# Weight loads as single steps, column means split up, block 1's norm and transposes closer together, and the exponential's table loaded ahead, in a fused graph-attention kernel

## The chip, the cores, the metric

One core of one Trainium2 chip. The metric is the device time of one launch in microseconds (us); smaller is better.

## The reference

128 graphs of 64 nodes with 768 features; two layers; the result is added to the input.

```python
h = relu(layernorm(x))
for l in range(2):
    m_left, m_right = h @ W_left[l].T, h @ W_right[l].T
    u_left, u_right = h @ m_left.T / sqrt(768), h @ m_right.T / sqrt(768)
    u = u_left * upper_triangle(adj) + u_right * lower_triangle(adj)
    e = exp(u) * adj
    attention = e / (sum(e, axis=2) + 1e-10)
    ctx = attention @ (h @ W_lin[l].T + b_lin[l])
    h = relu((ctx - mean) / (std + 1e-3) * ln_a[l] + ln_b[l])     # over features
out = x + h
```

## The kernel before

Each layer has two passes over 16 blocks of 512 tokens. Pass one multiplies by the left and the right weights and makes the scores; pass two multiplies by W_lin and forms the context. The products save matmuls by sums of blocks: fifteen products (ORDER) of sums of weight blocks and of token blocks (ts) into four PSUM tiles X, Y, Z, V, which ACT (ScalarE) or DVE (VectorE) read into m or hl. Pool (GpSimd) makes most of the sums. Nine raw 256 KB blocks make up a weight matrix; W_lin and the bias have their column mean taken off, so that the later norm needs no mean.

The order of the instructions is set by hand in slots, two to a group of eight matmuls. A slot runs what is planned for it, or else the next entry of a list for idle time:

```python
    def run(slot):
        if slot in plan:
            for f in plan.pop(slot):
                f()
        elif idle:
            f = idle.popleft()
            if f is not None:
                f()
```

The weights and the column means (t is the weight matrix in its nine blocks):

```python
        for s, (i, j) in RAW.items():
            nc.sync.dma_start(t[s], v[:, j * K2:(j + 1) * K2, i * D:(i + 1) * D])
        ...
            def means(blocks=blocks, m=m):
                for n, s in enumerate(blocks):
                    nc.vector.reduce_sum(m[:, n], t[s], axis=mybir.AxisListType.X)
                nc.vector.tensor_add(m[:, 0], m[:, 0], m[:, 1])
                nc.vector.tensor_add(m[:, 0], m[:, 0], m[:, 2])
                nc.vector.tensor_scalar_mul(m[:, 0], m[:, 0], 1.0 / H)
```

While block u is multiplied, block u+1 is prepared: statistics, norm, transposes into xb, a store of xb to memory (h) and a reload of it transposed (ht), then the row loads of block u+2 and an adjacency:

```python
            todo = transpose_rows(l, u, sp)          # statistics, norm, transposes, store
            todo.append(lambda: load_h(1, l, u))     # ht <- h
            if u + 1 < NB:
                todo.append(lambda: load_rows(l, u + 1, sp))
            todo.extend(softmax(u - 2) if u > 1 else [])
            todo.append(lambda: load_adj(u))
```

All these transfers go out from one queue (SP, SyncE) in program order. The slot at which one is written down sets its place in that queue, and no more: it goes out when the transfers before it have gone, the eighth before it has landed (the last row load for block 2 went out at 80.61, and the reload, eight places ahead, had landed at 80.59; of SP's 1238 transfers none went out before the eighth ahead of it had landed), and its own data are there (the reload went out at 73.44, and the store that it reads had landed at 73.29).

Of the kernel before, what the change touches and what calls it, by code (L numbers as in the profile page):

```python
# [17 lines left out]
def kernel(  # L18
# [27 lines left out]
    P = 128  # L46
# [69 lines left out]
    def load_w(l, kind):  # L116
        v = SRC[kind][l].rearrange("(c p) o -> p c o", p=P)
        t = W[l, kind] = [wpool.tile([P, K2, D], F32, name=f"w_{kind}_{s}") for s in range(len(ORDER))]
        for s, (i, j) in RAW.items():
            nc.sync.dma_start(t[s], v[:, j * K2:(j + 1) * K2, i * D:(i + 1) * D])  # L120

    def centre(l):

        t = W[l, "n"]
        for j in range(3):
            blocks = [s for s, (_, jj) in RAW.items() if jj == j]
            m = stat.tile([P, 3, K2], F32, name="wm", bufs=2)

            def means(blocks=blocks, m=m):
                for n, s in enumerate(blocks):  # L130
                    nc.vector.reduce_sum(m[:, n], t[s], axis=mybir.AxisListType.X)
                nc.vector.tensor_add(m[:, 0], m[:, 0], m[:, 1])
                nc.vector.tensor_add(m[:, 0], m[:, 0], m[:, 2])
                nc.vector.tensor_scalar_mul(m[:, 0], m[:, 0], 1.0 / H)

            idle.extend(none * (12 if j == 0 else 2))
            idle.append(means)
            for s in blocks:
                idle.extend(none * 3)
                idle.append(lambda s=s, m=m: nc.gpsimd.tensor_sub(  # L140
                    t[s], t[s], m[:, 0].unsqueeze(2).to_broadcast([P, K2, D])))

    def added(eng, o, sign, a, b):
        (eng.tensor_add if sign == "+" else eng.tensor_sub)(o, a, b)  # L144
# [114 lines left out]
    def transpose_rows(l, u, pool):  # L259

        key, xr, todo = (1, l, u), XR[l, u], []
        if l == 0:
            mv = stat.tile([P, Q, 2], F32, name="mv0", bufs=2)
            sd = stat.tile([P, Q], F32, name="sd0", bufs=2)
            rs = stat.tile([P, Q], F32, name="rs0", bufs=2)
            nb = stat.tile([P, Q], F32, name="nb0", bufs=2)

            def scale(q0, q1):
                nc.scalar.activation(sd[:, q0:q1], mv[:, q0:q1, 1], AF.Sqrt, bias=eps_in)
                nc.vector.reciprocal(rs[:, q0:q1], sd[:, q0:q1])  # L270
                nc.vector.scalar_tensor_tensor(nb[:, q0:q1], mv[:, q0:q1, 0], -1.0, rs[:, q0:q1],
                                               op0=ALU.mult, op1=ALU.mult)

            def norm(q):
                nc.scalar.activation(xr[q], xr[q], AF.Relu, bias=nb[:, q:q + 1], scale=rs[:, q:q + 1])

            stats = [lambda q=q: mean_var(mv[:, q, :], [xr[q][:, :HH], xr[q][:, HH:]]) for q in range(Q)]
            norms = [lambda q=q: norm(q) for q in range(Q)]
            if u:
                for f in stats + [lambda: scale(0, Q)] + norms:  # L280
                    todo.extend([f, None])
            else:
                scales = [lambda q=q: scale(q, q + 1) for q in range(Q)]
                todo.append(stats[0])
                for q in range(Q):
                    todo.extend(stats[q + 1:q + 2] + [scales[q], norms[q]])
        if (l, u) == (0, 0):
            ht = HT[key] = big.tile([P, C, T], F32, name="ht")

            def turn(c0):  # L290
                p = ps_aux.tile([P, 2, T], F32, name="aux")
                for c in range(2):
                    for q in range(Q):
                        nc.tensor.transpose(p[:, c, q * P:(q + 1) * P],
                                            xr[q][:, (c0 + c) * P:(c0 + c + 1) * P], ident)
                for c in range(2):
                    nc.scalar.copy(ht[:, c0 + c, :].rearrange("p (a g s) -> p g a s", a=4, g=2),
                                   p[:, c].rearrange("p (g a s) -> p g a s", a=4, g=2))

            for c in range(0, C, 2):  # L300
                todo.append(lambda c=c: turn(c))
            todo.append(lambda: nc.sync.dma_start(KEPT[l][u], ht))
            return todo

        xb = pool.tile([P, H // 32, Q, 32], F32, name="xb", bufs=1)

        def store():
            to = KEPT[l][u].rearrange("(b i) c t -> i c b t", b=4)
            for a in range(4):
                nc.sync.dma_start(to[:, :, :, a * P:(a + 1) * P],  # L310
                                  xb[a * 32:(a + 1) * 32].rearrange("i (c b) q j -> i c b (q j)", b=4))

        for q in range(Q):
            todo.append(lambda q=q: nc.vector.transpose(
                xb[:, :, q, :], xr[q].rearrange("p (b j) -> p b j", j=32)))
            todo.append(None)
        todo.append(store)
        return todo

# [6 lines left out]
    def pass_one(l, aside):  # L326
        with tc.tile_pool(name=f"one{l}", bufs=2, reuse_waits="tile") as sp:
# [106 lines left out]
            if l == 0:  # L434
                load_rows(0, 0, sp, (nc.sync, nc.scalar))
                warm = stat.tile([P, 1], F32, name="warm", bufs=1)
                nc.scalar.activation(warm, eps_in, AF.Sqrt)
                load_w(0, "l")
                load_w(0, "r")
                for f in transpose_rows(0, 0, sp):  # L440
                    if f:
                        f()

                t, w = deque(sums_t((1, 0, 0), nc.vector)), deque(sums_w(0, "l", nc.vector))
                needs = ("twww", "t", "wt", "ttwww", "wwww", "w", "tw", "t", "ww", "ww", "", "t", "t", "t", "t")
                for i, what in enumerate(needs):
                    for f in [(t if c == "t" else w).popleft() for c in what]:
                        if i < 3:
                            f()
                        else:  # L450
                            just.setdefault(i - 3, []).append(f)
                assert not t and not w
            load_adj(0)
            load_rows(l, 1, sp)
            if l == 0:
                cols.extend([column("a_col", ln_a[0]), column("b_col", ln_b[0])])
            for u in range(NB):
                slot = 0
                if u == 0:
                    if l == 0:  # L460
                        rs = sums_w(0, "r", nc.gpsimd)

                        def hold():

                            t = stat.tile([P, 1], F32, name="hold", bufs=1)
                            nc.gpsimd.tensor_copy(t, M[0][:, 0, 4, 0, :1])

                        put(16, hold)
                        for n in range(0, len(rs), 3):
                            put(17 + n // 3, *rs[n:n + 3])  # L470
                    slot = 14
                if u + 1 < NB:
                    slot = put_all(slot, prepare(u + 1))
                    nxt = (1, l, u + 1)
                else:
                    put(8, lambda: load_h(2, l, 0))
                    slot = put_all(9, softmax(u - 1) + none * 4 + affine(2, l, 0))
                    nxt = (2, l, 0)
                assert slot <= 47
                put_sums_t(nxt, max(slot, 40), 2 if slot <= 40 else 1, 30)  # L480
                if u in aside:
                    aside[u]()
                for k in range(2):
                    project(u, k, just if k == 0 and u == 0 else {})
                assert not plan
# [15 lines left out]
    def bias(l):  # L501
# [4 lines left out]
            row(f"b{i}", b_lin[l], i * D, (i + 1) * D, t[:, to])  # L506
        bm = stat.tile([P, 3], F32, name="bm", bufs=1)

        def centred():
            nc.vector.reduce_sum(bm, t[:, :3], axis=mybir.AxisListType.X)  # L510
            nc.vector.tensor_add(bm[:, 0:1], bm[:, 0:1], bm[:, 1:2])
            nc.vector.tensor_add(bm[:, 0:1], bm[:, 0:1], bm[:, 2:3])
            nc.vector.tensor_scalar_mul(bm[:, 0:1], bm[:, 0:1], -1.0 / H)
            nc.vector.tensor_scalar_add(t[:, :3], t[:, :3], bm[:, 0:1])

        def combined():
            nc.vector.tensor_add(t[:, 1], t[:, 1], t[:, 0])
            nc.vector.tensor_add(t[:, 3], t[:, 1], t[:, 2])
            for n in (0, 2):
                nc.vector.tensor_scalar_mul(t[:, n], t[:, n], -1.0)  # L520

        later([centred, combined], 6)
        return t

    AHEAD = []
# [158 lines left out]

    def one_aside(l):
        def begin():
            load_w(l, "n")
            centre(l)
            later(sums_w(l, "n", nc.gpsimd), 3)
            rows["bias", l] = bias(l)  # L690
# [1 line left out]

    def two_aside(kind):
        def begin():
            load_w(1, kind)
            later(sums_w(1, kind, nc.gpsimd), 4)
        return begin

    pass_one(0, {1: one_aside(0)})
# [32 lines left out]
```

## Time and profile before

| | before |
|---|---|
| time, median of the first 3 runs | 2802.0 us (2799.4 to 2802.6) |
| PE busy, of a profiled span of 2803.0 us | 2755.9 us |
| a block of pass one without a hole | 56.1 us |
| a slot | 0.86 us |

PE (TensorE) is busy nearly throughout, so what counts is where it stands still. A way of reading: block u's score matmuls come in one burst (tile aux) at the head of block u+1's work, so the distance from one burst to the next is the time of one block, and whatever is above 56.1 us is a hole. A burst is 192 matmuls with 192 weight loads, 384 instructions in 4.2 us. PE's program is fetched while it runs: the instruction queue (q8 of the page) moved 149 packets of 16.4 KB, and the trace holds 38111 instructions of PE, its sequencer's included. That makes blocks of some 256 instructions, an estimate that takes all of q8 for PE's; by it a burst uses up more than one of them. An "issue" wait is one for which the profile shows no semaphore.

### The profile page before, as it was taken

How to read it: one execution, taken by the hardware profiler on the slowest of the kernel's cores; microseconds unless marked ns; L12 is line 12 of the kernel's file. 1: busy time of each engine (PE TensorE's matmuls, PEld its weight loads, DVE VectorE, ACT ScalarE, POOL GpSimd, SP SyncE). 2: the span in 40 equal slices, each digit the busy share in tenths (PEclk: the TensorE clock that was granted, in tenths of full speed). 3: DMA queues.
4: the chain of work that ended last, by engine and by line, in shares of the span. 5: the costliest groups of instructions: out<-in, count | busy, mean ns of one | idle time of the engine just before them, and what ended most of it. 6: DMA issues, size and time to landing. Idle time of an engine off the chain costs nothing.

```text
span 2803.0 us, 46102 instructions
## 1 busy us (share of the span) xinstructions
PE 2755.9 (98%) x18712; PEld 2342.4 (84%) x18712; DVE 1340.9 (48%) x2223; ACT 838.7 (30%) x1452; POOL 1190.1 (42%) x935
## 2 busy tenths in 40 slices
PE   7999999999999999999999999999999999999997
PEld 6788888888888888888788888888888888888885
DVE  6454554454544332232345434443444335666666
ACT  2123222322131244444522221212122214545443
POOL 3343333222322556555333353223222335887875
PEclk9999999999999999999999999999999999999999
DMA  5633343234322243343563432343234204555654
GB/s 155 164 78 74 94 115 87 74 88 119 88 74 76 98 141 117 106 130 106 149 160 97 120 79 74 91 119 85 74 85 118 69 25 145 162 169 158 184 162 125
DMA packets 234068, 310.80 MB, mean 111 GB/s; under 512 B 54144, under 2 KB 184448, under 8 KB 225664
## 3 DMA queue, kind: packets, MB, share of 16 engines
q1 hardware_dynamic: 233568, 307.06, 40.0%
q8 instruction: 149, 2.44, 0.4%
q10 hardware_dynamic: 288, 0.79, 0.1%
q14 instruction: 63, 0.52, 0.1%
HBM read 202.91 MB, written 104.86 MB: 110 GB/s over the span
## 4 chain that ended last, share of the span: by engine, by line
PE 94%; DVE 2%; DMA 1%; ACT 1%; issue 1%; SPq 0%; POOL 0%; DVEq 0%; ACTq 0%; POOLq 0%
PE X L366 23%; PE V L366 15%; PE X L637 12%; PE Y L366 11%; PE Z L366 8%; PE V L637 8%; PE Y L637 6%; PE aux L392 5%; PE Z L637 4%; PE aux L564 3%; DVE m L144 1%; DMA ht<-h 0%; DMA h<-xb 0%; ACT ht L255 0%; DVE w_l L144 0%
## 5 line engine op out<-in xcount | busy, mean ns | idle before, releaser
L144 POOL TENSOR_TENSOR ts<-ht 128x512 f32<-128x512 f32 x441 | 585.7, 1340 | 1242.1 <-DMA ht<-h 555.7
L189 ACT ACTIVATE m<-X 128x512 f32<-128x512 f32 x256 | 152.7, 596 | 1117.1 <-PE X L366 589.5
L144 POOL TENSOR_TENSOR ts<-ht,ts 128x512 f32<-128x512 f32 x189 | 248.9, 1325 | 152.8 <-PE X L637 75.9
L144 DVE TENSOR_TENSOR m<-m,V 128x512 f32<-128x512 f32 x256 | 174.4, 681 | 271.9 <-PE V L366 271.9
L144 DVE TENSOR_TENSOR m<-m,X 128x512 f32<-128x512 f32 x256 | 163.8, 682 | 250.2 <-PE X L366 249.5
L366 PE MATMUL X<-ts,w_l 128*128 128x256 f32 x1024 | 246.6, 384 | 6.0 <-DVE w_l L144 2.1
L637 PE MATMUL X<-w_n,ts 128*128 128x256 f32 x1024 | 244.2, 380 | 0.9 <-ACT hl L189 0.6
L366 PE MATMUL X<-ts,w_r 128*128 128x256 f32 x1024 | 242.1, 379 | 0.2 <-ACT m L189 0.2
L144 DVE TENSOR_TENSOR m<-m,Z 128x512 f32<-128x512 f32 x128 | 88.0, 688 | 318.3 <-ACT m L189 257.3
L366 PEld LDWEIGHTS X<-ts,w_l 128*128 128x128 f32 x1024 | 194.2, 192 | 38.5 <-DVE m L144 4.6
L637 PEld LDWEIGHTS X<-w_n,ts 128*128 128x128 f32 x1024 | 191.6, 190 | 32.2 <-DVE hl L144 2.3
L366 PEld LDWEIGHTS X<-ts,w_r 128*128 128x128 f32 x1024 | 192.2, 190 | 29.6 <-ACT m L189 0.6
L255 ACT ACTIVATE ht<-ht,b_col,a_col 128x512 f32<-128x512 f32 x192 | 144.1, 808 | 142.9 <-DMA ht<-h 142.9
L637 PE MATMUL Y<-w_n,ts 128*128 128x256 f32 x768 | 182.4, 379 | 0.0
L366 PE MATMUL Y<-ts,w_l 128*128 128x256 f32 x768 | 181.8, 380 | 0.0
L366 PE MATMUL Y<-ts,w_r 128*128 128x256 f32 x768 | 181.4, 379 | 0.0
L189 ACT ACTIVATE hl<-X 128x512 f32<-128x512 f32 (+1 forms) x136 | 77.9, 573 | 329.4 <-PE X L637 320.0
L366 PEld LDWEIGHTS Y<-ts,w_l 128*128 128x128 f32 x768 | 146.4, 191 | 20.0
L637 PEld LDWEIGHTS Y<-w_n,ts 128*128 128x128 f32 x768 | 145.9, 190 | 19.8
L366 PEld LDWEIGHTS Y<-ts,w_r 128*128 128x128 f32 x768 | 145.9, 190 | 19.8
L603 POOL TENSOR_TENSOR z<-z,b 128x768 f32<-128x768 f32 x64 | 115.4, 1816 | 94.9 <-DVE z L600 94.9
L144 DVE TENSOR_TENSOR hl<-hl,X 128x512 f32<-128x512 f32 (+1 forms) x136 | 83.1, 653 | 147.2 <-PE X L637 139.8
(106 smaller groups left out, 4684.8 us busy)
## 6 DMA issues: line engine op xcount, KB each, us to landing
ht<-h SPq DMA_DIRECT2D x63, 1536.0 KB, 7.2
h<-xb SPq DMA_DIRECT2D x124, 384.0 KB, 6.8
z<-z SPq DMA_DIRECT2D x128, 192.0 KB, 2.9
x<-z SPq DMA_DIRECT2D x128, 192.0 KB, 8.4
xr<-in_x_dram SPq DMA_DIRECT2D x128, 192.0 KB, 3.7
out_dram<-xr SPq DMA_DIRECT2D x128, 192.0 KB, 2.6
x<-in_x_dram SPq DMA_DIRECT2D x120, 192.0 KB, 8.4
adj<-in_adj_dram SPq DMA_DIRECT2D x64, 128.0 KB, 2.8
```

Of the source, the lines that this page charges most:

```text
L144: (eng.tensor_add if sign == "+" else eng.tensor_sub)(o, a, b)
L189: nc.scalar.activation(to(o), p, AF.Copy, scale=1.0 if sign == "+" else -1.0)
L255: nc.scalar.activation(ht, ht, AF.Relu, bias=cols[1][:, c:c + 1], scale=cols[0][:, c:c + 1])
L366: nc.tensor.matmul(p[:, g], w[ORDER[i][0]][:, c, g * P:(g + 1) * P], b()[t][:, c, :], start=(new and g == c == 0), stop=(c == K2 - 1), ski ...
L392: nc.tensor.matmul(p[h * S + e:h * S + e + 32, q, e:e + 96], ht[:, c, b * S + e:b * S + e + 32], mb[:, e:e + 96], start=(c == 0), stop=(c ...
L564: nc.tensor.matmul(cx[k][i, m, :HH], at[j, q, :], hl[j, q, m * HH:(m + 1) * HH], start=True, stop=True)
L603: nc.gpsimd.tensor_add(zs[k], zs[k], rows["b"])
L637: nc.tensor.matmul(p[:, n], b[t][:, c, r * P:(r + 1) * P], w[s][:, c, :], start=(i in FIRST and i not in PRELOAD and n == c == 0), stop=(c ...
```

## The change

Its intent: to take four kinds of clump out of the schedule. Weight loads go one by one into idle slots instead of nine in a row; the three reductions of a column mean and the bias's steps get a slot each; block 1, which is prepared in a hurry, loses the empty slots between its norms and its transposes; the exponential's table in layer 1 is loaded by a dummy activation ahead of its first use.

```diff
     def load_w(l, kind):
-        for s, (i, j) in RAW.items():
-            nc.sync.dma_start(t[s], v[...])
+        return [lambda s=s, i=i, j=j: nc.sync.dma_start(t[s], v[...]) for s, (i, j) in RAW.items()]
...
-            idle.extend(none * (12 if j == 0 else 2))
-            idle.append(means)
+            def mean_of(m=m, mean=mean):
+                nc.vector.reduce_sum(mean, m.rearrange("p n c -> p c n"), axis=mybir.AxisListType.X)
+                nc.vector.tensor_scalar_mul(mean, mean, 1.0 / H)
+            idle.extend(none * (6 if j == 0 else 2))
+            for n, s in enumerate(blocks):
+                idle.append(lambda ...: nc.vector.reduce_sum(m[:, n], t[s], axis=mybir.AxisListType.X))
+            idle.append(mean_of)
...
-                for f in stats + [lambda: scale(0, Q)] + norms:
+                for f in stats + [lambda: scale(0, Q)]:
                     todo.extend([f, None])
+                for f in norms:
+                    todo.extend([f] + none * (u > 1))
...                                                  # after each transpose
-            todo.append(None)
+            todo.extend(none * ((l, u) != (0, 1)))
...                                                  # pass one, layer 1
+                warm = stat.tile([P, 1], F32, name="warm", bufs=1)
+                put(8, lambda: nc.scalar.activation(warm, eps_in, AF.Exp))
...                                                  # bias
-        later([centred, combined], 6)
+        later([mean, centred, combined, lambda: negated(0), lambda: negated(2)], 3)
...                                                  # pass one, then pass two
-            load_w(l, "n")
+            later(load_w(l, "n"), 1)
...
-            load_w(1, kind)
-            later(sums_w(1, kind, nc.gpsimd), 4)
+            later(load_w(1, kind), 1)
+            later(sums_w(1, kind, nc.gpsimd), 3)
```

(Not shown: in `bias`, two additions of single columns become one small reduction, and the two negations become functions of their own.)

More of the change, by code (lines that the diff above doesn't have):

```diff
@@ L118, in load_w @@
         t = W[l, kind] = [wpool.tile([P, K2, D], F32, name=f"w_{kind}_{s}") for s in range(len(ORDER))]
-        for s, (i, j) in RAW.items():
-            nc.sync.dma_start(t[s], v[:, j * K2:(j + 1) * K2, i * D:(i + 1) * D])
+        return [lambda s=s, i=i, j=j: nc.sync.dma_start(t[s], v[:, j * K2:(j + 1) * K2, i * D:(i + 1) * D])
+                for s, (i, j) in RAW.items()]
     def centre(l):
@@ L127, in centre @@
             m = stat.tile([P, 3, K2], F32, name="wm", bufs=2)
-            def means(blocks=blocks, m=m):
-                for n, s in enumerate(blocks):
-                    nc.vector.reduce_sum(m[:, n], t[s], axis=mybir.AxisListType.X)
-                nc.vector.tensor_add(m[:, 0], m[:, 0], m[:, 1])
-                nc.vector.tensor_add(m[:, 0], m[:, 0], m[:, 2])
-                nc.vector.tensor_scalar_mul(m[:, 0], m[:, 0], 1.0 / H)
-            idle.extend(none * (12 if j == 0 else 2))
-            idle.append(means)
+            mean = stat.tile([P, K2], F32, name="wmm", bufs=2)
+            def mean_of(m=m, mean=mean):
[3 more added lines that the diff above has]
+            for n, s in enumerate(blocks):
+                idle.append(lambda n=n, s=s, m=m: nc.vector.reduce_sum(m[:, n], t[s], axis=mybir.AxisListType.X))
+            idle.append(mean_of)
             for s in blocks:
                 idle.extend(none * 3)
-                idle.append(lambda s=s, m=m: nc.gpsimd.tensor_sub(
-                    t[s], t[s], m[:, 0].unsqueeze(2).to_broadcast([P, K2, D])))
+                idle.append(lambda s=s, mean=mean: nc.gpsimd.tensor_sub(
+                    t[s], t[s], mean.unsqueeze(2).to_broadcast([P, K2, D])))
     def added(eng, o, sign, a, b):
@@ L437, in pass_one @@
                 nc.scalar.activation(warm, eps_in, AF.Sqrt)
-                load_w(0, "l")
-                load_w(0, "r")
+                for f in load_w(0, "l") + load_w(0, "r"):
+                    f()
                 for f in transpose_rows(0, 0, sp):
@@ L456, in pass_one @@
                 cols.extend([column("a_col", ln_a[0]), column("b_col", ln_b[0])])
+            else:
+                warm = stat.tile([P, 1], F32, name="warm", bufs=1)
+                put(8, lambda: nc.scalar.activation(warm, eps_in, AF.Exp))
             for u in range(NB):
@@ L507, in bias, with mean @@
         bm = stat.tile([P, 3], F32, name="bm", bufs=1)
+        bs = stat.tile([P, 1], F32, name="bs", bufs=1)
+        def mean():
+            nc.vector.reduce_sum(bm, t[:, :3], axis=mybir.AxisListType.X)
+            nc.vector.reduce_sum(bs, bm, axis=mybir.AxisListType.X)
         def centred():
-            nc.vector.reduce_sum(bm, t[:, :3], axis=mybir.AxisListType.X)
-            nc.vector.tensor_add(bm[:, 0:1], bm[:, 0:1], bm[:, 1:2])
-            nc.vector.tensor_add(bm[:, 0:1], bm[:, 0:1], bm[:, 2:3])
-            nc.vector.tensor_scalar_mul(bm[:, 0:1], bm[:, 0:1], -1.0 / H)
-            nc.vector.tensor_scalar_add(t[:, :3], t[:, :3], bm[:, 0:1])
+            nc.vector.tensor_scalar_mul(bs, bs, -1.0 / H)
+            nc.vector.tensor_scalar_add(t[:, :3], t[:, :3], bs)
         def combined():
@@ L518, in combined, with negated @@
             nc.vector.tensor_add(t[:, 3], t[:, 1], t[:, 2])
-            for n in (0, 2):
-                nc.vector.tensor_scalar_mul(t[:, n], t[:, n], -1.0)
-        later([centred, combined], 6)
+        def negated(n):
+            nc.vector.tensor_scalar_mul(t[:, n], t[:, n], -1.0)
+        later([mean, centred, combined, lambda: negated(0), lambda: negated(2)], 3)
         return t
```

## The prediction

> **What bounds the kernel now.** I read the page first: which engine is full, and what the chain that ended last is made of.
>
> ```profile
> PE 2755.9 (98%) x18712; PEld 2342.4 (84%) x18712; DVE 1340.9 (48%) x2223; ACT 838.7 (30%) x1452; POOL 1190.1 (42%) x935
> ...
> PE 94%; DVE 2%; DMA 1%; ACT 1%; issue 1%; SPq 0%; POOL 0%; DVEq 0%; ACTq 0%; POOLq 0%
> ```
>
> TensorE is busy for 98% of the span and makes 94% of the chain. No part of the change touches a matmul: the built programs have the same PE instructions in the same order. So only holes in PE can be won, and 2803.0 - 2755.9 = 47 us is all the idle time there is. The view of waits for PE says whose they are (total, times, longest):
>
> ```profile
> PE aux L294 <- ACT x L275: 12.1, 4, 8.7
> PE V L366 <- DVE m L144: 3.9, 3, 1.5
> PE Z L366 <- issue: 3.1, 1, 3.1
> ...
> PE X L366 <- POOL ts L144: 2.1, 1, 2.1
> ...
> PE X L366 <- DVE m L144: 1.2, 1, 1.2
> ```
>
> The largest is the start, which the change leaves alone. The others are single events. To find them I took the chain in order of time and measured from one burst of score matmuls (aux) to the next, one burst per block of pass one:
>
> ```profile
> 83.97 4.10 PE aux L392 x192
> ...
> 146.18 4.10 PE aux L392 x192
> ...
> 203.58 4.10 PE aux L392 x192
> ...
> 259.68 3.60 PE aux L392 x168
> ```
>
> A good block takes 259.68 - 203.58 = 56.1 us. The distance from block 1's burst to block 2's is 62.2 (6.1 too long), the next 57.4 (1.3 too long). By the same view the one from 372.30 to 430.19 is 57.9 (1.8), in layer 1 those from 1464.47 to 1522.41 (1.8) and from 1747.79 to 1805.01 (1.1). Pass two repeats every 29.2 us almost without a hole. Four lines show what is inside: the timelines of PE, DVE and ACT and the stretch from 91 to 98 us (PE, PEld, DVE, ACT, POOL busy; clock; DMA share; GB/s).
>
> ```profile
> 92.44 1.65 PE L366 MATMUL Z<-ts,w_l 128*128 128x256 f32 x3 [3.10 <-issue]
> ```
> ```profile
> 91.00:98.00 7.00, 5.56 (x13) 4.48 (x14) 2.92 (x7) 1.06 (x2) 4.80 (x5) 0.51 0.70 241
> ```
> ```profile
> 194.37 1.19 DVE L133 TENSOR_TENSOR wm<-wm 128x2 f32<-128x2 f32 x1
> ```
> ```profile
> 1481.89 1.28 ACT L412 ACT_TABLE_LOAD   x1
> ```
>
> In block 1 PE stands 3.1 us with no semaphore to blame, after five of eight matmuls, and then runs at half clock. In the second a tiny addition for the column means takes 1.19 us on DVE, in front of PSUM reads. In the third the exponential's table is loaded in the middle of a block.
>
> [...] queue 8 moved 2.44 MB in 149 packets, 16.4 KB each. [...] a 2.1 us hole at 81.97 left the clock at 1.00. [...] the load took 1.28 us here, and exp began 0.02 us after it[...].
>
> **The change part by part.**
>
> *Norm and transposes of block 1 closer.* Four empty slots go among the norms and four among the transposes (a slot is 0.86 us, half a group of 1.73 us). The norms ran back to back anyway (ACT, 49.65 to 53.44), held by late statistics. The last transpose ended at 62.56; DVE is free from 52.5 on, needs 4 x 0.97 us and lets one PSUM read in, so it can end near 57.4, 5.15 us earlier. Behind it stands a chain of transfers: the store issued at 62.58 landed at 73.29, the reload of ht issued at 73.44 landed at 80.59, Pool's first sum began at 80.66, and PE waited 2.11 us for it, to 81.97. Five us of lead remove this wait and the restart: **2.35 us** (X can begin at 79.87 and the burst at 81.6 instead of 83.97).
>
> *Weight loads one by one.* Read packet by packet, the fetch for the PE block that block 1's burst uses up started at 89.99 and took 1.02 us; PE went on 1.43 us later. In four blocks without DMA load that fetch starts 1.1 to 1.7 us after the burst begins; here it would have been about 85.3. It was 4.7 us late: it stood behind transfers issued before it (the weight load issued at 83.35 landed at 89.75, the next at 90.53). The 3.1 us, and 14 matmuls at 0.427 instead of 0.216 us after it (3.0 us), make block 1's 6.1.
> The name of this part promises more than the program does. SP issues when its own queue lets it: nothing ties a load to the slot. In the built program the three bias rows and six of the nine loads still stand directly behind block 1's adjacency and go out at once; only three fall behind block 2's. So I work it out: all of SP's stream moves 5.15 us forward, PE's burst 2.35. The fetch is asked for near 82.95. The last adjacency lands at 89.34 - 5.15 = 84.2, the bias rows add 3 x 0.35, two weight loads 2 x 0.66: the fetch starts near 86.3, ends 87.3, PE goes on near 88.7, and needs it at 89.34 - 2.35 = 87.0. A wait of 1.7 us is left[...]. Worth (3.1 - 1.7) + 3.0 = **4.4 us**. In pass two and layer 1 the loads cost no PE time before (no hole beside them), so nothing there.
>
> *Column means in single steps.* Per third of the matrix three reductions (0.6 us each) stay, two tiny additions and a scaling become one reduction and a scaling: 6 DVE instructions fewer, in all 8 of 2223 with the bias. What counts is the clump: from 191.61 to 195.76 DVE did 4.15 us without reading PSUM, and V waited 0.93 us at 196.41. Split: **1.2** of that block's 1.3 us. The bias (0.94 + 3 x 0.16 + 0.62, five instructions in one slot at 393.31) stood between transposes and cost V 1.43 us at 400.6. Split and one block later, two additions (0.85 us) still stand before a transpose; counting DVE's work from 391.84 on gives V's read ending at 399.6 against 399.17 wanted: 0.45 left, **1.3 us** of 1.8. In layer 1 the bias additions (1755.39 to 1756.68) delayed a store and reload of ht; they move to late slots: **0.9** of 1.1.
>
> *Exponential's table ahead.* The load delayed exp, the product with exp waited 2.5 us on DVE, a PSUM read stood behind it, and X waited 1.2 us at 1485.89. Early in layer 1's block 0 ACT is idle 2.85 us between reads and hides 1.28: **1.5** of 1.8.
>
> Sum: 2.35 + 4.4 + 1.2 + 1.3 + 0.9 + 1.5 = 11.65 us; I take 0.5 off for new small holes. 2802.0 - 11.2 = **2791 us**, 0.4% less.
>
> **Rivals.** *The fetch still waits long.* Six loads and three bias rows still go out with the burst. If the fetch is again over 4 us late, 3.1 us and the half clock stay: 2795. If, on the contrary, the lead takes it past the backlog, there is no wait: 2789. For the first speaks that DMA is full throughout (share 1.08 from 80 to 90); for the second that bias rows are smaller.
> *The single steps fill slots that are already full.* Three reductions now stand at slots 1, 3 and 5 of block 2 beside the statistics: between the reads of Z and Y DVE then has 0.69 + 2 x 0.6 + 2 x 1.1 = 4.1 us of work where two groups give 3.46. That makes a read 1.2 us late, but that PSUM bank is next written four groups on. If I misjudge such clumps in three or four blocks: 2794 to 2796.
> *Loads that come later make a consumer wait in order.* The last three loads stand behind block 2's adjacency, near 135; DVE reduces them near 144 after block 2's burst at 139. They should be there by 139. They can also delay block 2's fetch, about 1 us with 1.3 to spare. If a reduction waits, DVE stands and PE with it: 2 to 4 us back.
>
> **Range and chances.** All removable holes together are about 14 us (2788), and with none of the fetch's gain and two misjudged clumps it is 2797. Runs of the kernel before spread over 3.1 us. So 2786 to 2797. Two per cent are 56 us, more than all of PE's idle time, so faster by 2% can't come from this: 1%. Slower by 2% would need a transfer or an order gone badly wrong: 0.5%.
>
> **What would show it.** Right: no PE wait for Pool's ts near 80; the burst of block 1 near 81.6; the "issue" wait of Z at 1 to 2 us and clock 1.00 after it; distances between bursts near 57.8, 56.2, and for the three others 56.1 to 56.6; no table load beside exp in layer 1. Wrong: half clock again near 90; ht landing later than 76; a new wait of PE for DVE's m in block 2 or 3; DVE waiting for a weight load; more than 50 us of PE idle.

## The result

The changed kernel took 2792.4 us (median of 4 runs, 2790.6 to 2793.3) against 2801.0 (4 runs) of the kernel before, and 2791.3 (5 runs) against 2801.7 (9 runs) when it was run again. The ratios are 0.9968 (95% interval 0.9951 to 0.9986) and 0.9961 (0.9947 to 0.9974). A ratio is the mean time of one kernel's fast runs over that of the other's of the same rounds, so not quite the ratio of the medians quoted.

The page of the changed kernel, busy times and chain:

```profile
PE 2751.3 (99%) x18712; PEld 2340.8 (84%) x18712; DVE 1340.8 (48%) x2215; ACT 837.8 (30%) x1453; POOL 1191.5 (43%) x935
...
PE 95%; issue 1%; DVE 1%; POOL 1%; DMA 1%; ACT 1%; SPq 0%; DVEq 0%; ACTq 0%; POOLq 0%
```

The work is the same; the span is 11.4 us shorter than that of the first trace of before. Its view of waits for PE (us in total, times, longest):

```profile
PE aux L297 <- ACT x L276: 12.3, 4, 8.9
...
PE Z L369 <- issue: 1.5, 1, 1.5
PE V L369 <- DVE m L145: 1.5, 1, 1.5
...
PE X L369 <- POOL ts L145: 1.1, 1, 1.1
```

Of three waits of V for DVE one is left, in block 0, which the change does not touch. X's wait for DVE's m in layer 1 is gone. The wait for Pool is 1.1 us, not gone. The issue wait has halved. The chain of the changed kernel in order of time, its first bursts:

```profile
83.17 4.10 PE aux L395 x192
...
141.07 4.10 PE aux L395 x192
...
197.16 4.10 PE aux L395 x192
...
253.26 3.60 PE aux L395 x168
```

141.07 - 83.17 = 57.9 us instead of 62.2, and 56.1 instead of 57.4 for the next. PE's timeline after the burst, and the stretch from 91 to 98 us:

```profile
90.08 0.92 PE L369 MATMUL Z<-ts,w_l 128*128 128x256 f32 x3 [1.54 <-issue]
```
```profile
91.00:98.00 7.00, 7.00 (x34) 6.15 (x34) 3.82 (x11) 3.28 (x6) 4.04 (x5) 1.00 0.04 13
```

The clock stays at 1.00, and DMA is quiet (share 0.04) where it was at 0.70. Which part of the change did that? SP's timeline around the burst shows the order in which the transfers went out (start, us of the whole row):

```profile
68.02 0.35 SPq L249 DMA_DIRECT2D ht<-h  x1
68.46 11.65 SPq L244 DMA_DIRECT2D x<-in_x_dram  x8
80.50 1.31 SPq L341 DMA_DIRECT2D adj<-in_adj_dram  x2
81.86 1.55 SPq L506 DMA_DIRECT2D bias<-in_b_lin_dram  x3
83.46 3.16 SPq L119 DMA_DIRECT2D w_n<-in_w_lin_dram  x6
```

Six of nine weight loads still go out in one run of 3.2 us, beside the burst (83.17 to 87.27): "one by one in free slots" holds in the program's text, not in time.

### The profile page after: what moved, and what is told of

Same layout as the page of the kernel before. It is cut to its first block, busy times and chain, and to the rows that moved or that the text cites. A ratio compares the mean times of both kernels' runs of the same rounds, so it can differ in the third digit from the quotient of the medians.

```text
span 2791.6 us, 46094 instructions
## 1 busy us (share of the span) xinstructions
PE 2751.3 (99%) x18712; PEld 2340.8 (84%) x18712; DVE 1340.8 (48%) x2215; ACT 837.8 (30%) x1453; POOL 1191.5 (43%) x935
## 4 chain that ended last, share of the span: by engine, by line
PE 95%; issue 1%; DVE 1%; POOL 1%; DMA 1%; ACT 1%; SPq 0%; DVEq 0%; ACTq 0%; POOLq 0%
PE X L369 23%; PE V L369 15%; PE X L648 12%; PE Y L369 12%; PE Z L369 8%; PE V L648 8%; PE Y L648 6%; PE aux L395 5%; PE Z L648 4%; PE aux L575 3%; POOL w_r L145 1%; DVE wm L409 0%; DMA x<-in_x_dram 0%; DMA w_r<-in_w_right_dram 0%; DMA w_l<-in_w_left_dram 0%
## 5 line engine op out<-in xcount | busy, mean ns | idle before, releaser
L145 POOL TENSOR_TENSOR ts<-ht,ts 128x512 f32<-128x512 f32 x189 | 249.3, 1327 | 154.7 <-PE X L648 76.9
```

The costliest lines, as they stand in the source:

```text
L145: (eng.tensor_add if sign == "+" else eng.tensor_sub)(o, a, b)
```

## The experiments

Eleven runs. First the four parts each alone on the kernel before, then both kernels again, then one part left out and mends. The table puts their traces side by side: the wait of PE for Pool ahead of block 1's burst, the issue wait after it, and the time from burst to burst (start to start; blocks are counted by the burst that opens the stretch; "L1" is layer 1). Two rows are read packet by packet from the traces: how long after the burst's start the instruction fetch that it needs begins, and how long block 1's reload of ht takes from issue to landing. Two runs, late_loads and late2_gap2, stand in the text only.

| us | before | before again | close | loads | steps | table | after | after again | at once | gap | late2 |
|---|---|---|---|---|---|---|---|---|---|---|---|
| wait for Pool | 2.1 | 1.8 | 0 | 1.6 | 1.5 | 1.5 | 1.1 | 0 | 0.9 | 0 | 0 |
| issue wait | 3.1 | 2.6 | 1.4 | 2.2 | 2.6 | 2.4 | 1.5 | 0.5 | 1.2 | 1.2 | 0 |
| fetch begins after | 6.1 | 5.8 | 4.5 | 5.2 | 5.6 | 5.6 | 4.6 | 3.6 | 3.1 | 4.1 | 2.1 |
| reload of ht takes | 7.2 | 6.8 | 7.9 | 6.8 | 6.9 | 6.7 | 11.8 | 10.1 | 11.6 | 7.0 | 9.0 |
| 1 to 2 | 62.2 | 59.0 | 57.7 | 58.6 | 59.0 | 58.7 | 57.9 | 56.9 | 57.6 | 57.6 | 56.1 |
| 2 to 3 | 57.4 | 57.6 | 57.5 | 56.1 | 56.5 | 57.3 | 56.1 | 56.1 | 56.1 | 56.1 | 56.1 |
| 6 to 8 | 114.0 | 114.2 | 114.4 | 113.1 | 112.4 | 114.4 | 113.2 | 113.3 | 113.1 | 113.2 | 113.0 |
| L1, 1 to 2 | 57.9 | 57.9 | 58.1 | 57.9 | 57.7 | 56.6 | 56.3 | 56.6 | 56.3 | 56.3 | 56.3 |
| L1, 6 to 8 | 113.7 | 114.0 | 113.4 | 112.6 | 112.6 | 112.9 | 112.9 | 112.9 | 113.1 | 112.6 | 112.6 |
| median time | 2801 | 2801 | 2797.2 | 2795.8 | 2798.1 | 2799.5 | 2792.4 | 2791.3 | 2793.0 | 2792.4 | 2789.7 |

Single traces carry chance: small issue waits of 0.2 to 0.7 us inside other bursts come and go, so a difference under 0.5 us in one cell says nothing.

### Only the closer norm and transposes

```diff
 # on the kernel before
-                for f in stats + [lambda: scale(0, Q)] + norms:
+                for f in stats + [lambda: scale(0, Q)]:
                     todo.extend([f, None])
+                for f in norms:
+                    todo.extend([f] + none * (u > 1))
...
-            todo.append(None)
+            todo.extend(none * ((l, u) != (0, 1)))
```

> Only the closer norm and transposes of block 1, on the kernel before; all nine weight loads and the bias rows still go out at once behind block 1's adjacency. My theory: the instruction fetch that PE needs after block 1's score burst waits behind the transfers issued before the burst began, so what helps it is how far the transfers' stream moves ahead of PE, not how many loads follow. Then this part alone brings most of block 1's 5.1 us: burst at 83 instead of 84, fetch starting near 87.7, the issue wait 1 to 2 us instead of 3.1, no half clock, and 4.5 to 5.5 us off the span (2795.5 to 2796.5). Rival (the change's own intent): nine loads in a row hold the fetch up; then the wait stays at 3 us or grows to over 4, because the burst comes earlier than before, half clock stays, and only 0 to 1 us is won. The holes near 196, 400, 1486 and 1784 stay in both.

Measured: 2797.2 us, ratio 0.9985 (0.9971 to 0.9999), some 4 us, a little under the 4.5 to 5.5 that I had expected. From its waits for PE:

```profile
PE Z L368 <- issue: 1.4, 1, 1.4
...
PE X L368 <- DVE m L144: 1.2, 1, 1.2
```

There is no wait for Pool any more, and with all nine weight loads and the bias still sent at once the issue wait is 1.4 us, as in the full change. The rival (more loads, longer wait) is out. What followed the burst in the queue made no wait of 3 us here; how far the queue had got by then is what this run changed.

### Only the weight loads as single steps

```diff
 # on the kernel before
-            load_w(l, "n")
+            later(load_w(l, "n"), 1)
...
-            idle.extend(none * (12 if j == 0 else 2))
+            idle.extend(none * (6 if j == 0 else 2))
...
-            load_w(1, kind)
-            later(sums_w(1, kind, nc.gpsimd), 4)
+            later(load_w(1, kind), 1)
+            later(sums_w(1, kind, nc.gpsimd), 3)
```

> Only the weight loads as single steps (with the shorter pause ahead of the column means), on the kernel before. My theory: the bias rows and six loads still go out at once beside the burst at 84, and the fetch stands behind what was issued before it; the wait stays 2.5 to 3.1 us with half clock after it, and the kernel gains 0 to 0.7 us. Rival (intent): three loads fewer beside the burst and small bias rows first let the fetch through: wait under 1.5 us, no half clock, 4 us or more off the span.

Measured: 2795.8 us, ratio 0.9983 (0.9970 to 0.9995). Of the fetch, the wait is nearer my theory than the rival, but outside the range of either: 2.2 us where I had written 2.5 to 3.1 and the rival had under 1.5; and the half clock that I had expected did not come. And the kernel gained near 5 us where I had written 0 to 0.7, for a reason that I had not thought of: loads in the idle list push everything behind them to other slots. The column means of the three thirds are still three clumps, but they stand elsewhere: they begin at 141, 180 and 210 us instead of 116, 156 and 192. Two lines of the second one in DVE's timeline:

```profile
180.13 1.86 DVE L131 TENSOR_REDUCE wm<-w_n 128x2 f32<-128x512 f32 x3
...
182.09 0.16 DVE L133 TENSOR_TENSOR wm<-wm 128x2 f32<-128x2 f32 x1
```

Its second tiny addition takes 0.16 us; in the clump that made the hole of the kernel before (at 192) it took 1.19. None of the three makes PE wait for DVE now, and the hole from burst 2 to 3 is gone (56.1), without any splitting. The bias's clump has moved too: 6 to 8 loses 1 us, L1 6 to 8 loses 1.1 us. So most of the time credited to "loads" is won by moving DVE's work. (The edit also shortens two pauses in the list; the run cannot tell their share of the shift from that of the loads' entries.)

### Only the column means and the bias in single steps

```diff
 # on the kernel before: the changed kernel's centre() and bias(), with the pause of 12 kept
-            idle.append(means)
+            for n, s in enumerate(blocks):
+                idle.append(lambda ...: nc.vector.reduce_sum(m[:, n], t[s], axis=mybir.AxisListType.X))
+            idle.append(mean_of)
...
-        later([centred, combined], 6)
+        later([mean, centred, combined, lambda: negated(0), lambda: negated(2)], 3)
```

> Only the column means and the bias in single steps, on the kernel before. My theory: block 1 stays as it was (wait 2.1 for Pool, 3.1 issue, half clock); the DVE holes near 196 (0.9 us) and 400 (1.4 us) and the late reload near 1780 in layer 1 go: distances between bursts of 57.4, 57.9 and 57.2 fall to 56.1 to 56.7, together 2.5 to 3.3 us off the span. Rival: PE's reads only wait elsewhere, as DVE does nearly the same work: under 1 us.

Measured: 2798.1 us, ratio 0.9986 (0.9974 to 0.9999), about 3 to 4 us. Block 1 stays (issue wait 2.6), the three stretches fall to 56.5, 112.4 and 112.6. Its waits of V for DVE:

```profile
PE V L367 <- DVE m L145: 1.7, 2, 1.5
```

The two that are left are block 0's 1.5 us and a new one of 0.2 us near 168, where a reduction now stands. For the holes this is as expected, and the rival (they only move) holds for 0.2 us; the half clock that I had expected in block 1 did not come.

### Only the table ahead

```diff
 # on the kernel before, pass one, layer 1
+            else:
+                warm = stat.tile([P, 1], F32, name="warm", bufs=1)
+                put(8, lambda: nc.scalar.activation(warm, eps_in, AF.Exp))
```

> Only the exponential's table loaded in layer 1's block 0, on the kernel before. My theory: the wait of X for DVE's m near 1486 (1.2 us) goes, the distance between bursts there falls from 57.9 to 56.3, 1.6 us off the span, nothing else moves. Rival: the transposes and score reads that stand before it on DVE are what delays the read, and the wait stays: under 0.4 us.

Measured: 2799.5 us, ratio 0.9993 (0.9981 to 1.0006): by the clock alone not clear of nothing. The trace decides. In its chain in order of time:

```profile
1457.97 3.59 PE aux L392 x165
1514.56 4.10 PE aux L392 x192
```

These are 56.6 us apart; the kernel before takes 57.9 in two traces of two. No wait of X for DVE's m is left. In the changed kernel ACT's timeline has the load here, in layer 1's block 0, where nothing waits for it:

```profile
1409.29 1.28 ACT L463 ACT_TABLE_LOAD   x1
```

### Both kernels again

> The changed kernel again, for a second trace and a closer interval. Block 1's reload of ht took 11.8 us in the first trace where 7.2 was expected, so PE still waited 1.1 us for Pool's first sum. If that is chance (one of the DMA engines held up in that execution), it lands in 7 to 9 us here, the wait is 0 and block 1's burst begins near 81.7. If it is the rule (the instruction fetch that starts with the reload, or the row loads behind it), it takes 10 to 12 us again. The issue wait after the burst stays at 1 to 2 us, clock 1.00; span 7 to 11 us under the kernel before.

> The kernel before again, for a second trace. If the 3.1 us issue wait with half clock after block 1's burst is the rule it is here again within 0.5 us, block 1 taking 61.5 to 62.5 us; if it was chance, block 1 takes 57 to 59.

The changed kernel again: 2791.3 us; reload of ht in 10.1 us, fetch beginning 0.1 us after its issue, but no wait for Pool this time, and an issue wait of 0.5, less than the 1 to 2 expected. The kernel before again (one look, 2801.0 us), waits for PE and the stretch from 91 to 98:

```profile
PE Z L366 <- issue: 2.6, 1, 2.6
...
PE X L366 <- POOL ts L144: 1.8, 1, 1.8
```
```profile
91.00:98.00 7.00, 7.00 (x34) 6.16 (x33) 3.76 (x10) 2.79 (x5) 3.41 (x4) 1.00 0.47 157
```

The issue wait is the rule (2.4 to 3.1 us in four traces with the old order up to there). The half clock behind it is not: it came in one trace of those four, the one with the longest wait, 3.1 us. PE's clock in that trace was already at half between 91.3 and 92.4 us, inside the hole that began at 89.34 (1.00 until 91.2). The view of that stretch, PE busy 0.00, clock 0.50:

```profile
91.30:92.40 1.10, 0.00 (x0) 0.00 (x0) 0.00 (x0) 0.00 (x0) 1.10 (x2) 0.50 1.09 379
```

Block 1's burst starts at 82.5 here and at 83.9 there, but most of that lies before block 1: block 0's V began at 50.91 here and at 51.97 there, and in the first trace of the changed kernel at 52.18.

### The weight loads at once, all else changed

```diff
 # on the changed kernel
-        return [lambda s=s, i=i, j=j: nc.sync.dma_start(t[s], v[...]) for s, (i, j) in RAW.items()]
+        for s, (i, j) in RAW.items():
+            nc.sync.dma_start(t[s], v[...])
+        return none * len(RAW)
```

(Not shown: the two calls, which put eight more empty entries behind it.) The empty entries keep every slot as it was: in the traces PE, DVE, ACT and Pool run the same instructions in the same order as in the changed kernel, and SP's order alone differs.

> The changed kernel with the weight loads sent at once again, everything else in its place: only the transfer queue's order differs. My theory: the fetch after block 1's burst stands behind what was issued before the burst, and three loads more behind it don't matter; loads in front instead of bias rows cost some 0.3 to 0.8 us: issue wait 1.4 to 2.3 us against 1.5 and 0.5 in the two traces of the changed kernel, block 1 at 57.7 to 58.6, the span within 1 us of the changed kernel, no other block moves. Rival: sending the loads one by one is what shortened the wait: 2.4 to 3.1 us again, 2 us or more slower.

Measured: 2793.0 us (2791.9 to 2793.3), ratio 0.9968 (0.9955 to 0.9981). From its waits:

```profile
PE Z L370 <- issue: 1.2, 1, 1.2
...
PE X L370 <- POOL ts L146: 0.9, 1, 0.9
```

The issue wait is within that of the changed kernel (1.5 and 0.5), if by another road: the fetch began only 3.1 us after the burst, but took 2.3 us itself, where it took 0.9 to 1.2 in all the other traces. The time is 0.6 to 1.7 us above the changed kernel's two medians. They were run at other times. Sending the loads one by one is worth 2 us at most, and perhaps nothing.

### The loads really kept away from the burst

```diff
 # on the changed kernel
-            later(load_w(l, "n"), 1)
+            fs = load_w(l, "n")
+            if l == 0:
+                for n, f in enumerate(fs[:6]):
+                    put(29 + n, f)               # behind block 2's row loads in the queue
+                idle.extend(none * 12)
+                fs = fs[6:]
+            later(fs, 1)
```

and the bias rows are loaded much later, just ahead of their use.

> The changed kernel with the weight loads of layer 0 really kept off block 1's burst: the first six stand behind block 2's row loads in the transfer queue, the bias rows much later. My theory: the fetch after block 1's burst finds the queue nearly empty, starts 1 to 1.7 us after the burst begins, the issue wait of 1.5 us goes, block 1 takes 56.1 to 56.4 instead of 57.9: 1.5 us less than the changed kernel, the fastest of all. Rival: the fetch is slow for another reason (the row loads and the adjacency before it): wait unchanged. Risk: the loads now lie before block 2's burst and hold up its fetch: then block 2 gets longer by what block 1 wins.

> The kernel with the loads kept off block 1's burst, mended: layer 1's bias rows are loaded where the changed kernel loads them, so that DVE doesn't wait for them near 1778 (1.2 us). Block 1 at 56.1 with no issue wait, the block from 1735 on at 56.5 to 56.8; 1 to 1.8 us faster than the changed kernel.

The first version: block 1 took 56.1 us with no issue wait, as expected, and still the time was 2791.5 (ratio 0.9960, 0.9948 to 0.9973), as fast as the changed kernel, because I had moved layer 1's bias rows too. Its DVE timeline:

```profile
1776.30 0.95 DVE L522 TENSOR_REDUCE bm<-bias 128x3 f32<-128x768 f32 x1 [6.53 <-DMA bias<-in_b_lin_dram]
```

DVE waited for a load that came too late, and PE stood 1.2 us behind it. Mended (late2 in the table): 2789.7 us (2788.7 to 2791.4), ratio 0.9958 (0.9945 to 0.9970). PE's timeline around block 1's burst has no hole:

```profile
79.38 4.17 PE L395 MATMUL aux<-m,ht 128*32 128x96 f32 x192
83.47 1.99 PE L369 MATMUL Z<-ts,w_l 128*128 128x256 f32 x8
```

This shows what held the fetch up: take the transfers away from the burst and the wait is nil, in both versions (0.4 us in the run with both mends below); in late2 the fetch begins 2.1 us after the burst, where it began after 4.6 and 3.6 in the changed kernel. The mended version has the lowest median; all its five runs lie below the five of each of the two kernels run in its rounds without this mend (at once and gap2). The changed kernel itself ran in other calls, and its ratio of 0.9961 (0.9947 to 0.9974) is not apart from 0.9958.

### The reload two microseconds later

```diff
 # on the changed kernel, transposes
         for q in range(Q):
+            if (l, u, q) == (0, 1, 3):
+                todo.extend(none * 2)
```

> The changed kernel with block 1's last transpose two slots later, so that its store and the reload of ht are issued about 2.2 us later (reload near 70 instead of 68), after the instruction fetch that starts near 68 and no longer with it. If the fetch is what made the reload take 10.1 to 11.8 us (three traces, fetch within 0.2 us of the issue; 6.7 to 7.9 us in six traces without that), it takes 6.7 to 8 us here and lands at 77 to 78, as early as before or earlier although issued later, and PE doesn't wait for Pool's sum or waits under 0.3 us: 0 to 1 us faster than the changed kernel. If the row loads issued right behind it, or DMA bandwidth, were the cause, it takes 10 to 12 us again, lands near 81 and PE waits about 2 us more.

The reload's row in the DMA view of a stretch around its issue (KB, us from issue to landing), in the kernel before, the changed kernel, and this one:

```profile
ht<-h SPq DMA_DIRECT2D x1, 1536.0 KB, 7.2
```
```profile
ht<-h SPq DMA_DIRECT2D x1, 1536.0 KB, 11.8
```
```profile
ht<-h SPq DMA_DIRECT2D x1, 1536.0 KB, 7.0
```

Issued at 69.35 instead of 68.02, it landed at 76.3 instead of 79.8, and PE did not wait for Pool. That fits the theory, but the expectation overlooked a case against its rule. In the run with the closer transposes alone the fetch (68.17) and the issue (68.19) also stand within 0.2 us, and the reload took 7.9 us:

```profile
ht<-h SPq DMA_DIRECT2D x1, 1536.0 KB, 7.9
```

Read packet by packet, the reloads of layer 0's pass one in all thirteen traces say: in 15 the fetch began 0.01 to 0.35 us after the issue, and they took 7.4 to 11.8 us (median 10.1); in 4 it began up to 0.07 us before the issue, and they took 7.9 to 8.5; the other 187 took 6.3 to 8.9 (median 7.1), those with a fetch in their middle no longer than the rest (median 7.0). In layer 1 two reloads with a fetch 0.12 and 0.16 us behind the issue took 6.9 and 7.0. So a fetch that begins just behind the issue goes with a slow reload in layer 0, not always and not by a fixed amount; what else it takes stays open. As to the kernel, the time is 2792.4 (ratio 0.9966, 0.9954 to 0.9979), no gain: with the burst earlier and the queue behind the reload later, the issue wait is back at 1.2 us. The two mends pull against each other as long as loads stand beside the burst.

Both mends together:

> Both mends together, the candidate for the fastest: no issue wait in block 1 and no wait for Pool before it: 1.5 to 2.8 us faster than the changed kernel, near 2789.

2790.7 us (2789.9 to 2791.3), ratio 0.9960 (0.9946 to 0.9974): no wait for Pool, issue wait 0.4 us. Slower than late2 alone by 1 us, not faster as I had expected; in late2 Pool's sum came in time in spite of a reload of 9.0 us. What is left between the two is within what single executions differ by, and I leave it open.

## Why the prediction was right

The predicted 2791 with 2786 to 2797 held: 2792.4 and 2791.3. Most of its signs came too (issue wait, clock 1.00, the distances, no table load beside exp), but also one that it had set down as a sign of being wrong: ht landed at 79.8 and 76.9, later than 76, and in the first trace PE waited 1.1 us for Pool. "Within 2%" held too, for the reason given: all of PE's idle time was less than 2%. The steps, by the means of the traces that share the old arrangement of a part (four each, five for the table) against the two of the changed kernel:

- **Norm and transposes closer, 2.35 us predicted: about 1.2.** The transposes ended and the store went out as worked out (57.54 for 57.4), the reload at 68.02. The step that failed: the reload was to take its old 7.2 us and took 11.8 and 10.1; so the wait for Pool fell from a mean of 1.7 us to 0.55, not to 0. Its new place in time is the start of an instruction fetch, and 1.3 us later it took 7.0; but at the same place in the run with this part alone it took 7.9, so the fetch is likely a part of the cause and not shown to be all of it.
- **Weight loads, 4.4 us: 2.3 from burst 1 to 2, and not through the loads.** The mechanism (the fetch stands behind what was issued before it: it began 3.1 to 6.1 us after the burst with transfers beside it, 2.1 in late2) fits all runs, and moving the transfers away took the wait to 0; it was predicted at 1.7 and found at 1.5 and 0.5. (The prediction's own terms, 84.2 + 3 x 0.35 + 2 x 0.66, give 86.6 for the fetch's start and not 86.3, so a wait of 2.0 us.) But the 3.0 us for half clock came in one trace in four, so its mean share is 0.75 (in that trace the hole was 3.1 us long, and the clock was at half within 2.0 us of its beginning at 89.34, for 6.8 us in all; waits of 2.6 us in two other traces brought no half clock, nor did the changed kernel's 1.5; that 1.7 us would bring none was my estimate, from the 2.1 us hole at 81.97); and the credit belongs to the closer transposes, which alone bring the wait to 1.4. The loads by themselves leave it at 2.2: SP sends six of nine at once, as the prediction said.
- **Column means and bias: 1.2, 1.3 and 0.9 us predicted; 1.35, 1.0 and 0.6 found.** The remaining wait after the moved bias additions was to be 0.45 us; it is 0.13 (near 449). In layer 1 the late store alone does not make the hole: with the same late store and a reload of 7.6 us the table run has none to speak of, while the three traces with the late store and a reload of 8.7 to 9.0 us have it (it lands 30.1 to 30.7 us after the burst there, 29.0 in the table run); and the steps run, with an earlier store, has none in spite of a reload of 8.7. It took both. Splitting was not needed for the first: moving the clump, as the loads run did, took that hole away as well.
- **Table: 1.5 us, found 1.5.**
- **The 0.5 us for new holes:** 0.13 us near 449, and in the steps run 0.2 near 168. About right.

The parts add up to 1.2 + 2.3 + 1.35 + 1.0 + 0.6 + 1.5 = 8 us, against 8.6 and 10.4 by the medians. The sum of my terms, 11.2, came close to the 11.4 us between the first two traces partly because the first trace of before, from which I read them, held the half clock, which its other traces do not. (Its late start does not count: the first trace of the changed kernel started as late.) Two errors, the reload and the clock, pointed the same way, 1.2 and about 2 us. So the mechanisms held, but that the time came out within 1.4 us of 2791 is partly luck: the terms add up to 3 us more than the holes that the traces show filled. The 2.4 us between these 8 and the second pair of medians are not traced to a hole; they lie within the interval of its ratio, 7.3 to 14.8 us.

## What to carry to other kernels

Transfers put "in free slots" of a schedule were not spread in time here: nothing that they waited for tied them to the slots, and six of nine loads went out in one run of 3.2 us. So read the issuing queue's timeline, and put the load behind another transfer that is late by itself (in late2 six loads stood behind block 2's row loads and went out from 123.76 us on, and the burst at 79.38 had no wait behind it). In a kernel of 18712 matmuls PE's own instruction fetches are transfers too, 149 packets of 16.4 KB in the first trace: here block 1's burst of 384 short instructions went without a wait only when the transfers queued beside it had been moved away (0 us in late_loads and late2, 0.4 with both mends, 0.5 to 3.1 in the ten other traces). And before crediting a part of a change, undo that part with every other instruction in its place: here "single loads" alone won 5 us, most of it through what they pushed aside, and 2 us at most through themselves.
